# Four graph layers on 128 graphs, one core: a new order for fill and drain, the last transposition on TensorE, early statistics in the last layer

## Chip, cores and metric

One core of one Trainium2 chip. The metric is the device time in microseconds of one execution of the whole program; less is better.

## What is computed

`x` is (128 graphs, 128 nodes, 512 features) float32, `adj` a (128, 128) weighted adjacency shared by all graphs. Four layers follow each other, each with a residual and a layer normalisation `LN` over the 512 features:

```python
# layer 0
x = LN(x + (adj @ x) @ weight + bias)
# layer 1
q, k, v = x @ Wq.T, x @ Wk.T, x @ Wv.T
rel = adj.T * (q @ k.T)                       # per graph, 128 x 128
x = LN(x + (rel / norm(rel, axis=2)) @ v)
# layer 2
h = x @ W;  s1, s2 = h @ a[:512], h @ a[512:]
att = softmax(leaky_relu(s1[:, :, None] + s2[:, None, :], 0.2) * adj, axis=2)
x = LN(x + elu(att @ h + beta * h))
# layer 3: A = adj @ x, C = adj @ x + b; the maximum over the second index of relu(A + (C - A))
x = LN(x + relu(max over features of (adj @ x) + b))
```

In layer 3 the same adjacency stands for both weights, so what is added to `x` is one number per node and graph.

## The kernel before

The 128 graphs are worked in 32 groups of four. Nodes lie on the 128 partitions; a group's `x` is a 128 x (4, 512) tile. For each group the functions `layer0` to `layer3` put pieces of work, closures of a few instructions, into one list with a written time each (`emit`, `each`); the list is sorted by these times at the end, and that is the program order of all engines. The times are in slots, 28 for a group; the table `TABLE` holds them for an ordinary group, `FIRST` overrides them for groups 0 and 1, and `LAST` for the last three groups (29, 30, 31), there in microseconds counted from the start of group 31's middle product. The wrapper `InOrder` keeps each engine's instructions in program order, so an engine that waits holds up all that stands behind it in its queue. All instructions issued through the wrapper carry line 26 in the profile; tiles tell them apart.

The big products (256 or 512 wide) go through seven-product block multiplication: `left_factors` makes four sums of the left operand on GpSimd, `weight_blocks` four of the weight on VectorE, `product` takes seven steps of four 128x256 matmuls each (eight records in the profile), and after each step `out` moves a result off PSUM, ScalarE for steps 1, 6, 5 and 4 of a fresh target, VectorE for 2, 7 and 3 (order 1, 2, 6, 5, 7, 3, 4). Steps 6, 7 and 4 go on adding in the PSUM region of step 1, step 3 in that of step 5, so each waits for the one before to be read. Tiles of a product are `r_y` (layer 0), `r_m` (x times M, with M = Wq' Wk held in `m_qk`), `r_v` (values) and `r_z` (layer 2). Other tiles: `p_y` adj times x, `p_rel` scores, `p_o` attention output, `p_z` layer 2's gathered rows, `p_a` layer 3's products, each in one of three PSUM banks; `c` layer 2's result, `m` its exponential, `mx` and `top` layer 3's maximum, `mean` and `r` its shift and scale, `wa` the two weight rows with which VectorE forms layer 2's s1 and s2 (`dots`, tile `scr`).

Start (lines 95 to 230): SP loads `adj`, the four graphs of group 0, Wq, Wk, Wv and small tensors; ScalarE's queue loads `w0`, `bias` and `w2`. TensorE transposes `adj`, ScalarE copies it to `adjT`. `prepare_0` makes the factors of w0, `prepare_qk` forms M with 16 plain 128x512 matmuls (`p_m`), `prepare_v` transposes Wv (`p_wv`), `prepare_dots` and `prepare_rows` make `wa`, `prepare_2` the factors of w2.

In layer 1 `rel` is transposed by VectorE in 32x32 blocks and 16 transfers on SP (`turn_rel`, `move_rel`). In layer 3 (`squares`, `top`, `spread`, `shift`, `apply`) ScalarE takes the sum of squares of x, adds `top` to x with a running sum, VectorE turns both sums into mean and variance, GpSimd raises to -1/2, ScalarE applies and SP stores. In group 31 layer 2's product is direct (`direct`, tile `c`, one 128x512 accumulation of four matmuls for each graph), and normalisation and storing go graph by graph. In the last two groups (`late`) s2 is spread over partitions by four TensorE transposes (`p_s`), in the others by a DRAM round trip.

Of the kernel before, what the change touches and what calls it, by code (L numbers as in the profile page):

```python
# [29 lines left out]
def kernel(  # L30
# [41 lines left out]
    G = 4  # L72
    NG = B // G
    assert B % G == 0 and K == 4

# [11 lines left out]
    def on_all(row, n):  # L87

        return bass.AP(tensor=row.tensor, offset=row.offset, ap=[[0, P], [1, n]])
# [6 lines left out]
    def load(g):  # L96
        x1[g] = data.tile([P, G, D], FP, tag="x1", name=f"x1_{g}", bufs=3)
        if g == 0:
            for b in range(G):
                nc.sync.dma_start(x1[g][:, b, :], x[b])  # L100
        else:
            sync.dma_start(x1[g], x[g * G : (g + 1) * G].rearrange("b n d -> n b d"))

    load(0)
    w0_sb = const.tile([P, K, D], FP)
    nc.scalar.dma_start(w0_sb, w0.rearrange("(k p) f -> p k f", p=P))
    bias_sb = const.tile([P, D], FP)
    nc.scalar.dma_start(bias_sb, on_all(bias0, D))

    wq_sb = work.tile([P, K, D], FP, tag="tv", name="wq_sb")  # L110
# [6 lines left out]
    w2_sb = const.tile([P, K, D], FP)  # L117
    nc.scalar.dma_start(w2_sb, w2.rearrange("(k p) f -> p k f", p=P))
    a_sb = data.tile([P, 2, D], FP, tag="x3", name="a_sb")
# [6 lines left out]
    bias_halves = {0: bias_sb[:, :H], 2: bias_sb[:, H:]}  # L126
    dve.tensor_tensor(bias_halves[2], bias_halves[2], bias_halves[0], ALU.subtract)

# [12 lines left out]
    pe.transpose(pt[:, :P], adj_sb, ident)  # L141
    act.copy(adjT, pt[:, :P])
    adj_b = adj_sb[:, None, :].to_broadcast([P, G, P])
# [8 lines left out]

    def weight_blocks(w, name, keep=0):


        def blk(kh, ch):
            return w[:, 2 * kh : 2 * kh + 2, H * ch : H * ch + H]

        t = const.tile([P, 3 + keep, 2, H], FP, name=f"t_{name}")
        t2, t3, t4 = t[:, 0], t[:, 1], t[:, 2]  # L160
        t1 = t[:, 3] if keep else blk(0, 1)
        dve.tensor_tensor(t3, blk(1, 1), blk(0, 1), ALU.subtract)
        dve.tensor_tensor(t2, t3, blk(0, 0), ALU.add)
        dve.tensor_tensor(t4, blk(1, 0), t2, ALU.subtract)
        dve.tensor_tensor(t1, blk(0, 1), blk(0, 0), ALU.subtract)
        return {1: blk(0, 0), 2: blk(1, 0), 3: blk(1, 1), 4: t4, 5: t1, 6: t2, 7: t3}

    bw = {}

    def prepare_0():  # L170
        bw["0"] = weight_blocks(w0_sb, "0")

    def prepare_qk(c):

        pm = bank(f"p_m{c}")
        for e in range(K):
            pe.matmul(
                pm,
                wq_sb[:, e, c * P : (c + 1) * P],
                wk_sb[:, e, :],  # L180
                start=(e == 0),
                stop=(e == K - 1),
            )
        act.copy(m_qk[:, c, :], pm)
        if c == K - 1:
            bw["m"] = weight_blocks(m_qk, "m")

    def prepare_v(c):
        pv = bank(f"p_wv{c}")
        for e in range(K):  # L190
            pe.transpose(pv[:, e * P : (e + 1) * P], wv_sb[:, e, c * P : (c + 1) * P], ident)
        act.copy(wvT[:, c, :], pv)
        if c == K - 1:
            bw["v"] = weight_blocks(wvT, "v")

# [16 lines left out]
    def prepare_rows():  # L212

        for i in range(2):
            for k in range(K):
                pe.transpose(
                    wa[:, i, k * P : (k + 1) * P],
                    col[:, i, k : k + 1].to_broadcast([P, P]),
                    ident,
                )  # L220
        dve.tensor_reduce(wa_sum, wa, AX.X, ALU.add, negate=True)
        dve.tensor_scalar(beta_i, ident, beta_sb, None, op0=ALU.mult)

    def prepare_2():
        bw["2"] = weight_blocks(w2_sb, "2", 1)

# [10 lines left out]
    def row(at, step, n=G):  # L237
        return [at + i * step for i in range(n)]
# [18 lines left out]

    FIRST = {0: dict(turn=row(20.4, 0.3)), 1: dict(y=row(-9.5, 0.3))}

    LAST = {  # L260
        NG - 3: dict(
            exp=[0.8, 1.5, 2.2, 11.0], elu=[9.7, 12.3, 14.6, 17.2], norm2=[19.5],
            apply2=row(21.0, 0.8), widen=[24.5, 27.1, 29.7, 32.3], top=[25.5, 28.0, 30.6, 33.2],
            stats3=[27.0, 29.9, 32.2, 35.8], norm3=[42.0], apply3=row(44.0, 0.8), store=[47.4],
        ),
        NG - 2: dict(
            scale=[5.6], apply1=row(24.3, 0.8), spread=[6.9], leaky=[7.4], weighted=[9.0],
            greatest=[10.5], exps=[11.2], divide=[13.6], turn_att=[18.3], with_beta=[18.9],
            gather=row(36.7, 0.9), z_sums=row(39.95, 1.3),
            z_w=[40.0, 41.8, 43.5, 45.2, 47.0, 49.4, 51.1], exp=[51.5, 52.2, 56.2, 58.6],  # L270
            elu=row(56.9, 2.3), norm2=[66.1], apply2=row(67.7, 0.8), widen=row(73.0, 0.86),
            top=[73.7, 74.6, 78.0, 78.9], stats3=row(79.8, 0.9), norm3=[83.4],
            apply3=row(84.8, 0.8), store=[88.2],
        ),
        NG - 1: dict(
            m=[0.0, 1.73, 3.46, 5.2, 7.4, 9.1, 10.8], scores=row(12.7, 0.9), masked=[16.4],
            squares=[17.2], turn_rel=[17.1], move_rel=row(18.0, 0.1), inverse=[20.0], v=[16.7, 18.4, 21.0, 22.7, 25.3, 27.9, 30.5],
            attend=row(33.2, 0.86), residual=row(34.1, 1.65), norm1=[40.65], dots=row(40.7, 1.53),
            scale=[47.0], apply1=row(47.5, 0.8), spread=[48.9], leaky=[49.4], weighted=[51.0],
            greatest=[52.4], exps=row(53.2, 0.6), divide=row(53.9, 0.6),  # L280
            turn_att=row(54.4, 0.6), with_beta=row(54.9, 0.6), gather=[55.2, 56.1, 60.5, 65.0],
            z_w=[57.0, 61.5, 66.0, 69.5], exp=[60.6, 65.0, 69.6, 73.2],
            elu=[66.3, 68.8, 71.3, 75.5], norm2=[68.5, 71.0, 73.5, 77.7],
            apply2=[70.0, 72.5, 75.0, 79.4], widen=[77.0, 77.9, 78.8, 80.5],
            top=[83.5, 84.4, 85.3, 87.0], stats3=[86.1, 87.9, 88.8, 89.7],
            norm3=[86.9, 88.7, 89.6, 90.5], apply3=[88.3, 90.1, 91.0, 91.9],
            store=[89.2, 91.0, 91.9, 92.8],
        ),
# [59 lines left out]

    def product(at, name, mul, s, w, c, fresh, begin=None, before=None):

# [35 lines left out]
        for n, i in enumerate(ORDER):  # L386
            if before is not None and i in (1, 5):
                emit(at[n] - 0.7, fill, REGION[i])
            emit(at[n], step, i)
            emit(at[n] + 0.72, out, i)  # L390
# [46 lines left out]
    def layer0(g, t):  # L437
# [18 lines left out]
        if g > 0:  # L456
# [3 lines left out]
        product(  # L460
            t["y_w"], f"y_{g}", by_rows, s, "0", rows_of(lambda: x1[g]), False, before=bias_halves
        )
# [4 lines left out]
    def layer1(g, t):  # L467
# [69 lines left out]
        def turn_rel():  # L537
            s["relB"] = work.tile([P, 2, Q, 2 * P // Q], FP, tag="relB", name=f"relB_{g}")
            s["relT"] = work.tile([P, 2, 2 * P], FP, tag="relT", name=f"relT_{g}")
            for b in range(G):  # L540
# [3 lines left out]
                )  # L544

        def move_rel(a):
            n = P // Q
            for q in range(Q):
                sync.dma_start(
                    s["relT"][q * n : (q + 1) * n, :, 2 * a * n : 2 * (a + 1) * n],  # L550
                    s["relB"][a * n : (a + 1) * n, :, q, :],
                )
# [18 lines left out]
        def residual(b):  # L571
# [9 lines left out]
            )  # L581
            stats(s, f"1_{g}", b, x2[g][:, b, :])

# [40 lines left out]
        emit(t["squares"][0], squares)  # L624
        emit(t["turn_rel"][0], turn_rel)
        each(t["move_rel"], move_rel)
        emit(t["inverse"][0], inverse)
        product(t["v"], f"v_{g}", by_rows, s, "v", rows_of(lambda: s["v"]), True, begin_values)
        each(t["attend"], attend)
        each(t["residual"], residual)  # L630
        each(t["dots"], dots)
        emit(t["scale"][0], scale_dots)
# [7 lines left out]
    def layer2(g, t):  # L640
# [4 lines left out]
        def spread():  # L645
            if late:
                p = bank(f"p_s2_{g}")
# [134 lines left out]
        def elu(b):  # L782
            if b == 0:
                x3[g] = data.tile([P, G, D], FP, tag="x3", name=f"x3_{g}")
            x = x3[g][:, b, :]
# [31 lines left out]
    def layer3(g, t):  # L817
# [47 lines left out]
        def store(i):  # L865
            for b in range(i * n, i * n + n):
                sync.dma_start(out[g * G + b], x3[g][:, b, :])

        n = G // len(t["store"])
        each(t["widen"], widen)  # L870
        for b in range(G):
            emit(t["widen"][b] - 0.1, squares, b)
        each(t["top"], top)
        each(t["norm3"], spread)
        for i in range(len(t["norm3"])):
            emit(t["apply3"][i * n] - 0.1, shift, i)
        each(t["apply3"], apply)
        each(t["store"], store)


    emit(-1, prepare_0)
    each(row(14.0, 1.0), prepare_qk)
    each(row(18.0, 0.1), prepare_v)
    each(row(29.2, 1.8), prepare_dots)
    emit(40.7, prepare_rows)
    emit(61.0, prepare_2)
    for g in range(NG):
# [33 lines left out]
```

## Time and profile before

| | us |
|---|---|
| three runs | 2187.71, 2188.13, 2185.8 (median 2187.71) |
| the profiled execution | 2185.83, its span 2184.1 |
| PE busy, share of the span | 2149.5, 98% |
| DVE / ACT / POOL busy | 1552.1 / 1127.9 / 716.3 |
| chain that ended last | PE 94%, DVE 3%, ACT 2% |

Matmuls are pipelined, so the step from the start of one to the start of the next is what counts, and the durations in the table of groups are longer than that step. The page's slices of the span show PE at 9 tenths or more in all but the first and the last slice. The times below are from the start of the span.

### The profile page before, as it was taken

Reading aid. Unit: us, or ns where it says so; the run is one execution under the profiler, and the core shown is the slowest. Engines: PE = TensorE matmul, PEld = TensorE weight load, DVE = VectorE, ACT = ScalarE, POOL = GpSimd, SP = SyncE. Lnnn points to the kernel's source line nnn. Section 1 sums busy time; section 2 is a strip of 40 time slices with the busy share of each in tenths; the row PEclk is TensorE's granted clock in tenths of the full one; section 3 lists DMA queues with packets and bytes.
Section 4 is the critical chain, followed back from the end, with each engine's and each line's share of the span. In section 5 each row is a group of like instructions: output and inputs, shape, how many; then the busy total and the mean of one; then the engine's idle time right before and its main releaser. Section 6 shows DMA issues by size and latency. Waiting matters only on the chain.

```text
span 2184.1 us, 31923 instructions
## 1 busy us (share of the span) xinstructions
PE 2149.5 (98%) x10839; PEld 1814.6 (83%) x10839; DVE 1552.1 (71%) x3411; ACT 1127.9 (52%) x2510; POOL 716.3 (33%) x585
## 2 busy tenths in 40 slices
PE   8999999999999999999999999999999999999996
PEld 6888888888888888888888888888888888888873
DVE  3666777777767767767767777767777767677776
ACT  3235455555455555455554455554555554555557
POOL 1223333233333333233323333333332333342321
PEclk9999999999999999999999999999999999999998
DMA  4022222222222222322221323222322222322101
GB/s 170 6 58 50 67 73 68 57 57 63 71 74 68 54 59 60 75 70 73 54 57 60 75 66 78 54 52 65 74 67 61 64 55 70 73 68 56 38 25 58
DMA packets 363537, 138.82 MB, mean 64 GB/s; under 512 B 304624, under 2 KB 320112, under 8 KB 363376
## 3 DMA queue, kind: packets, MB, share of 16 engines
q1 hardware_dynamic: 362176, 134.43, 24.4%
q10 hardware_dynamic: 1200, 2.36, 0.3%
q8 instruction: 87, 1.43, 0.3%
q14 instruction: 74, 0.61, 0.1%
HBM read 55.38 MB, written 41.48 MB: 44 GB/s over the span
## 4 chain that ended last, share of the span: by engine, by line
PE 94%; DVE 3%; ACT 2%; issue 0%; POOL 0%; DMA 0%; ACTq 0%; DVEq 0%
PE r_y L26 17%; PE r_m L26 17%; PE r_v L26 17%; PE r_z L26 17%; PE p_y L26 5%; PE p_z L26 5%; PE p_rel L26 5%; PE p_o L26 5%; PE p_a L26 5%; DVE x L26 1%; ACT x L26 1%; PE p_m L26 1%; DVE st L26 1%; DMA w_sb<-in_L_gnn_weight_dram 0%; DVE t L26 0%
## 5 line engine op out<-in xcount | busy, mean ns | idle before, releaser
L26 ACT ACTIVATE x<-x,nmean,rstd 128x512 f32<-128x512 f32 x384 | 285.6, 807 | 41.3 <-DVE nmean L26 38.0
L26 DVE BATCH_NORM_STATS2 st<-x 128x6 f32<-128x512 f32 x384 | 263.0, 685 | 8.7
L26 POOL TENSOR_TENSOR rstd<-ve,mhalf 128x4 f32<-128x4 f32 (+1 forms) x99 | 108.9, 1100 | 334.4 <-DVE ve L26 334.4
L26 DVE TENSOR_TENSOR x<-r_y,x 128x512 f32<-128x512 f32 x224 | 152.2, 680 | 92.5 <-PE r_y L26 82.5
L26 ACT COPY yT<-p_y 128x512 f32<-128x512 f32 x128 | 75.0, 586 | 192.5 <-PE p_y L26 192.5
L26 DVE TENSOR_REDUCE mx<-p_a 128x1 f32<-128x512 f32 x128 | 88.2, 691 | 105.3 <-PE p_a L26 102.4
L26 DVE SCALAR_TENSOR_TENSOR scr<-x,wa 128x512 f32<-128x512 f32 x256 | 162.3, 679 | 0.0
L26 ACT ACTIVATE x<-x,mean,r 128x512 f32<-128x512 f32 x128 | 97.1, 808 | 108.4 <-DVE mean L26 108.4
L26 POOL TENSOR_TENSOR rn<-n,mhalf 128x4 f32<-128x4 f32 x32 | 32.6, 1017 | 347.5 <-ACT sq L26 347.5
L26 PEld LDWEIGHTS p_y<-adjT,x 128*128 128x128 f32 x1024 | 135.0, 194 | 8.9 <-ACT adjT L26 2.6
L26 PEld LDWEIGHTS p_z<-eT,x 128*128 128x128 f32 x1024 | 134.0, 192 | 7.9 <-issue 1.0
L26 PEld LDWEIGHTS p_rel<-xT,tT 128*128 128x128 f32 x1024 | 134.1, 191 | 7.4 <-DVE tT L26 0.8
L26 DVE TENSOR_TENSOR tT<-r_m,tT 128x512 f32<-128x512 f32 x96 | 66.3, 691 | 102.4 <-PE r_m L26 97.9
L26 ACT COPY tT<-r_m 128x512 f32<-128x512 f32 x128 | 75.6, 591 | 121.3 <-PE r_m L26 121.3
L26 PE MATMUL p_y<-adjT,x 128*128 128x128 f32 x1024 | 135.8, 277 | 2.1 <-ACT adjT L26 2.1
L26 PE MATMUL p_rel<-xT,tT 128*128 128x128 f32 x1024 | 134.9, 275 | 0.6 <-DVE tT L26 0.6
L26 PE MATMUL p_z<-eT,x 128*128 128x128 f32 x1024 | 134.7, 275 | 0.1
L26 ACT COPY zT<-p_z 128x512 f32<-128x512 f32 x128 | 73.8, 576 | 117.5 <-PE p_z L26 117.5
L26 PE MATMUL p_a<-x,adjT 128*128 128x512 f32 x256 | 126.3, 597 | 5.8 <-DVE mx L26 4.4
L26 POOL TENSOR_TENSOR s_y<-yT 128x512 f32<-128x512 f32 x32 | 41.1, 1284 | 276.1 <-ACT yT L26 276.1
L26 PE MATMUL p_o<-v,relT 128*128 128x512 f32 x256 | 130.5, 593 | 0.3 <-ACT v L26 0.3
L26 ACT COPY v<-r_v 128x512 f32<-128x512 f32 x128 | 74.1, 579 | 108.3 <-PE r_v L26 108.3
(135 smaller groups left out, 5214.7 us busy)
## 6 DMA issues: line engine op xcount, KB each, us to landing
out_dram<-x SPq DMA_DIRECT2D x128, 256.0 KB, 2.1
x<-in_x_dram SPq DMA_DIRECT2D x31, 1024.0 KB, 7.5
xT<-xB SPq DMA_DIRECT2D x480, 64.0 KB, 2.3
relT<-relB SPq DMA_DIRECT2D x512, 16.0 KB, 1.8
s<-s2d SPq DMA_DIRECT2D x30, 256.0 KB, 5.1
eBd<-eB SPq DMA_DIRECT2D x30, 256.0 KB, 2.0
eT<-eBd SPq DMA_DIRECT2D x120, 64.0 KB, 2.0
w_sb<-in_L_gnn_weight_dram ACTq DMA_DIRECT2D x1, 1024.0 KB, 5.7
```

What stands on the lines that cost most here:

```text
L26: return lambda *args, **kw: self.tc.keep_in_program_order(op(*args, **kw))
```

## The change

At the start: `bias` moves to SP's queue between the second and third graph, w2 to SP's behind Wv; VectorE instead of ScalarE copies `adjT`; eight matmuls of the identity follow adj's transposition (`p_warm`); the bias copy for the first product comes earlier (`lead`); M is formed by the seven-step product, with sums of Wq on GpSimd and factors of Wk on VectorE in a borrowed buffer; the factors of each weight are four pieces with times of their own; the preparation pieces and the pieces of groups 0 and 1 get new times; group 0's s2 is spread by TensorE. At the end: new times for the last three groups; group 31's `rel` is turned by four TensorE transposes and one ScalarE copy; its layer 1 statistics come after all four residuals; its layer 2 output takes the `xB` buffer; in groups 30 and 31 layer 3's statistics are taken of x itself, ahead of `top` (adding one number to a row moves its mean and not its variance), so ScalarE's squares and sums fall away, and `top` is formed on VectorE.

```diff
+                if b == 1:
+                    nc.sync.dma_start(bias_sb, on_all(bias0, D))
...
-    nc.scalar.dma_start(bias_sb, on_all(bias0, D))
...
-    nc.scalar.dma_start(w2_sb, w2.rearrange("(k p) f -> p k f", p=P))
+    nc.sync.dma_start(w2_sb, w2.rearrange("(k p) f -> p k f", p=P))
...
-    act.copy(adjT, pt[:, :P])
+    dve.tensor_copy(adjT, pt[:, :P])
+
+    warm = bank("p_warm")
+    for i in range(WARM):
+        pe.matmul(warm[:, :P], ident, ident, start=True, stop=True)
...
-    FIRST = {0: dict(turn=row(20.4, 0.3)), 1: dict(y=row(-9.5, 0.3))}
+    FIRST = {
+        0: dict(stats0=row(15.8, 0.02), norm0=[15.95], apply0=row(18.0, 0.1), turn=row(20.4, 0.3),
+                dots=row(57.8, 0.1), scale=[58.9], spread=[61.6]),
+        1: dict(y=row(-9.5, 0.3), y_sums=row(-4.0, 0.1), apply0=row(18.0, 0.1), turn=row(20.3, 0.3),
+                x_sums=row(22.5, 0.5)),
+    }
...
+        def turn_last():
+            p = bank(f"p_relT_{g}")
+            for b in range(G):
+                pe.transpose(p[:, b * P : (b + 1) * P], s["rel"][:, b, :], ident)
+            s["relT"] = work.tile([P, 2, 2 * P], FP, tag="relT", name=f"relT_{g}")
+            act.copy(
+                s["relT"].rearrange("p h (n j) -> p h j n", j=2),
+                p.rearrange("p (h j n) -> p h j n", h=2, j=2),
+            )
...
-            stats(s, f"1_{g}", b, x2[g][:, b, :])
+            if g < NG - 1:
+                stats(s, f"1_{g}", b, x2[g][:, b, :])
...
-            if late:
+            if late or g == 0:
...
+                    x3[g] = work.tile([P, G, D], FP, tag="xB", name=f"x3_{g}")
...
+        def top_late(b):
...
+            dve.tensor_reduce(mx, s["a", b], AX.X, ALU.max)
+            tp = s["top"][:, b : b + 1]
+            dve.tensor_scalar(tp, mx, b3_sb, 0.0, op0=ALU.add, op1=ALU.max)
+
+        def shift_late(i):
...
+            dve.tensor_tensor(m, s["mv"][:, sl, 0], s["top"][:, sl], ALU.add)
+            dve.tensor_tensor(m, s["top"][:, sl], m, ALU.subtract)
+            dve.tensor_tensor(m, m, s["r", i], ALU.mult)
...
+            each(t["stats3"], lambda b: stats(s, f"3_{g}", b, x3[g][:, b, :]))
+            each(t["norm3"], spread_early)
+            each(t["top"], top_late)
...
-    each(row(14.0, 1.0), prepare_qk)
-    each(row(18.0, 0.1), prepare_v)
-    each(row(29.2, 1.8), prepare_dots)
-    emit(40.7, prepare_rows)
-    emit(61.0, prepare_2)
+    weight_blocks(row(-1, 0), "0", w0_sb)
+    weight_blocks([11.85, 11.86, 12.85, 12.86], "k", wk_sb, 1, "x2")
+    qk = {"qT": wq_sb}
+    left_factors(row(12.0, 0.1), qk, "qT", "s_x", "q", 1)
+    product(row(14, 1, 7), "qk", by_rows, qk, "k", rows_of(lambda: m_qk), True)
+    weight_blocks([19.8, 19.81, 20.9, 20.91], "m", m_qk)
+    each(row(21.0, 0.1), prepare_v)
+    each([29.8, 30.4, 34.0, 34.5], prepare_dots)
+    weight_blocks(row(36.0, 1.0), "v", wvT)
+    emit(49.0, prepare_rows)
+    weight_blocks(row(72.3, 0.1), "2", w2_sb, 1)
```

Of the last groups' written times: group 29's last three `p_a` (`widen`) move from 27.1, 29.7, 32.3 to 54.9, 55.0, 59.3; group 30's `z_w` from 40.0 to 51.1 becomes 37.2 to 48.3; group 31's `elu` goes from 66.3, 68.8, 71.3, 75.5 to 56.5, 62.0, 67.5, 70.9 and its `top` from 83.5 to 87.0 to 69.86 to 77.0.

## The prediction

> **What bounds the kernel now.** First the busy time of each engine in three stages (columns: length, busy time of PE, PEld, DVE, ACT and POOL with instruction counts, granted clock, DMA share, GB/s):
>
> ```profile
> 0.00:160.00 160.00, 149.91 (x735) 122.02 (x736) 83.41 (x170) 48.57 (x99) 40.23 (x37) 0.99 0.26 79
> 160.00:2079.00 1919.00, 1918.74 (x9762) 1636.50 (x9761) 1395.82 (x3053) 1014.16 (x2262) 654.64 (x525) 1.00 0.26 64
> 2079.00:2184.10 105.10, 80.87 (x346) 56.08 (x344) 72.84 (x190) 65.16 (x149) 21.41 (x23) 0.93 0.09 34
> ```
>
> The reader is to see that TensorE idles 10.1 us in the fill, 0.3 us in 1919 us of steady work, and 24.2 us in the drain. The program order of groups 3 to 28 is the same in both kernels on every engine, so whatever TensorE gains before 160 us reaches the end undiminished, and only fill and drain can change. Next the start: granted clock by stage, TensorE's waits before 50 us, and the order of time.
>
> ```profile
> 6.00:9.00 3.00, 0.93 (x6) 0.54 (x5) 0.46 (x3) 1.55 (x2) 0.00 (x0) 1.00 0.95 302
> 9.00:12.00 3.00, 3.00 (x16) 3.00 (x15) 2.56 (x4) 0.76 (x2) 0.00 (x0) 0.50 1.05 405
> 12.00:13.00 1.00, 1.00 (x9) 1.00 (x9) 0.00 (x0) 0.41 (x1) 0.00 (x0) 0.80 1.05 389
> ```
> ```profile
> PE p_y L26 <- ACT adjT L26: 2.1, 1, 2.1
> PE p_wv L26 <- ACT wvT L26: 1.9, 1, 1.9
> PE r_y L26 <- ACT r_y L26: 1.2, 1, 1.2
> ```
> ```profile
> 6.43 0.39 ACTq L118 DMA_DIRECT2D w_sb<-in_L_gnn_W_dram  x1
> 6.85 1.28 ACT L26 ACT_TABLE_LOAD   x1 [6.85 <-DMA w_sb<-in_L_gnn_weight_dram]
> 8.14 0.27 ACT L26 COPY adjT<-p_adjT 128x128 f32<-128x128 f32 x1
> 8.46 5.47 PE L26 MATMUL p_y<-adjT,x 128*128 128x128 f32 x32 [2.07 <-ACT adjT L26]
> 27.29 13.90 PE L26 MATMUL p_m<-wk_sb,wq_sb 128*128 128x512 f32 x32
> ```
>
> ScalarE's third load (w2) waits until w0 has landed; behind it stand the table load and the adjT copy, and TensorE waits for that copy. It goes cold meanwhile: eight p_y records take 1.7 us at clock 0.50 and 0.87 later. Last the end, in order of time and in the chain of waits:
>
> ```profile
> 2141.94 0.68 DVE L26 SCALAR_TENSOR_TENSOR x<-c,x 128x512 f32<-128x512 f32 x1
> ...
> 2179.07 0.16 DVE L26 TENSOR_TENSOR mean<-mean,r 128x1 f32<-128x1 f32 x1 [0.59 <-POOL r L26]
> ```
> ```profile
> 2180.40 0.70 ACT x L26
> ```
>
> From the first ELU of group 30 (2141.94) to the last shift (2179.07) it is VectorE and ScalarE that set the time, 37.1 us; 5.0 us more pass until the end.
>
> **What the Trainium skill says.** "TensorE: Matmul & The Clock Gate", section "What's actually happening": half rate by default, full rate after about 3.4 us of sustained work. The trace agrees: 0.50 in 9 to 12 us, full from about 12.4, 3.9 us after p_y began. The same page, "Architectural detail", calls the queues of ACT and DVE strict FIFOs; the adjT wait above is one. "SBUF — State Buffer", section "SBUF: two separate sides", calls the port pair of VectorE and GpSimd an exclusive lock: the four factors of w2 at 111.9 us took 1.42, 1.64, 1.64 and 0.68 us with GpSimd running, against 0.69 alone.
>
> **Fill, part by part.** Prices are steps from start to start: one product step (eight records of 128x256) 1.725 us, eight 128x128 records 0.865, four transposes 0.43, two 128x512 records 0.86, a 128x512 copy on ACT 0.5 to 0.58, a sum on POOL 1.25, on DVE 0.61 to 0.73.
>
> 1. adjT by DVE (which idles until 8.5), w2 moved to SP, bias to SP between x[1] and x[2]. p_adjT ends at 6.39, adjT is there at about 6.7. The 16 warm records run 6.2 to 8.0 (0.108 each at the clock p_adjT had: its record took 0.27, as at full clock). x[0] had landed at 7.3 (it released SP's wv load), x[1] at 9.0. So p_y runs from 8.0 at full clock, paced by x: last block 10.6 to 11.5. Bounds: 0 to 1.9 us later if the clock drops all the same; bias in front of x[2] and x[3] at 390 GB/s costs x[3] at most 0.7.
> 2. The bias copy goes ahead of yT[3] (lead 4.4) and waits for bias; behind it on ACT is yT[3], for which POOL waits. In before bias landed at 8.5; now at 9 to 9.6; the copy's turn is 11.4: hidden. r_y starts at 11.95 (before 15.10) and ends 12.1 later at 24.05 (27.1).
> 3. M = Wq'Wk as a seven-step product: 12.1 instead of 13.8 (32 records by 0.43). Its sums on POOL (four by 1.25, 17.7 to 22.8, behind y's) and wk's factors on DVE (four by 0.7 to 1.64, between x sums) are done by 26.4, before their steps at 27.5 and later; wk landed at 18.5 before, 14 to 19 now.
> 4. p_y of group 1 goes inside this product, the turns of x and Wv alternate behind it: 3.46+1.73+1.73. Nine ACT copies by 0.58 feed three banks, TensorE waits about 1.1. x of group 1 (before: issued 13.84, landed 12.2 later) is needed at 32.7: hidden, though SP's loads now queue behind w0's landing. So r_m of group 0 starts at 24.05+19.0+1.1 = 44.1 (50.43).
> 5. r_m, r_y, r_v of groups 0 and 1 follow with the same work; wa (0.87) only moves; the turn of s2 for group 0 adds 0.43. The pauses of 1.34 (106.6), 1.73 (about 117) and 0.43 (123.9) go: group 0's dots now stand after tT's first sum, the four factors of w2 (6.4 with GpSimd) move past 132 us, where nmean of group 2 stands behind them; ScalarE cannot take that apply before 140.8 in any case (it copies v until then). Starts: r_m(1) 90.0 (97.23), r_y(2) 106.0 (114.50), r_v(2) 121.8 (132.69).
>
> Sum 10.9; some 15 handovers of 0.05 to 0.1 are left out, so I take **10.0**, bounds 6 and 11.
>
> **Drain, part by part**, on the clock of before (r_m of group 31 at 2079.06).
> 1. Two sums of tT now stand before the ELU on DVE: p_rel ends at 2095.4 (2096.25). Layer 3 of group 29 leaves r_v: four p_a by 0.86 and the pauses 0.16, 0.63, 0.56 go. rel by four transposes (0.43) and one ACT copy replaces 16 SP issues (10.9 us from 2099.6), which would land about 2112.5; p_o now starts at 2108.4 (2113.9). p_o ends 2111.9, r_z starts 2115.3 (2122.3).
> 2. Here some is given back. Statistics of all four blocks (four by 0.82) and rstd (1.02) stand before s_z on POOL: step 3 of r_z waits until 2120.0. Eight dots (4.9) stand before its second sum on DVE, four applies before its third copy on ACT: step 4 at 2122.2, step 5 at 2125.2 (0 to 1 more by the shared port; I take 0.4). The p_a of group 29 fills one gap. p_z of group 31 starts at 2131.6 (2139.5), the first ELU at 2134.0 (2141.94).
> 3. The tail on DVE: eight ELUs with statistics by 2.27 = 18.2, eight early statistics by 0.82 = 6.6, eleven maxima by 0.64 = 7.0 (three of group 29 moved here), eight tops by 0.2, five shifts by 0.6, group 29's small steps 1.0, other small ones 2.5: 39.9. Waits: the first ELU of group 31 stands on DVE before group 30's last two, and its exp stands on ACT behind a copy of p_z's third block, itself behind c_0 and two p_a (about 1.5); two statistics wait for an apply (0.4 and 0.9). 42.7 in all against 37.1, last shift at 2176.7 less 0.7 for small steps that overlap = 2176.0 (2179.07). Four applies instead of one then follow: end at 2176.0+4 by 0.72+3.0 (last apply's end 2181.1 to 2184.1) = 2181.9.
> The squares and sums that leave ACT (8 by 0.6+0.7+0.3 = 12.8) are worth little by themselves: ACT is no longer last. The output of group 31 in the xB buffer costs nothing: that buffer was last read by xT's transfers, tens of us before.
>
> Drain gain 2.2, bounds -3 and +9. Sum 12.2: the profiled span 2184.1 becomes 2171.9. The median of the runs stands 3.6 above that span; I take the difference from it: 2187.7-12.2 = **2175.5**.
>
> **Rivals.**
> A. The tail is not VectorE's: if the 7.9 us by which the first ELU comes earlier pass through (small steps overlap, statistics fill waits that exist anyway: before, DVE had some 7 us of waits there), 10+8 = 18: 2169.7. Against: the 12 us of work added to that tail exceed these waits.
> B. The fill gives half: clock cold through p_y (1.9), bias late, banks slower; 6, and nothing in the drain: 2181.7. For: the 405 GB/s of that stage leave DMA no slack.
> C. Slower: the tail's loops run one after another. Each block of group 31 goes DVE statistics, POOL 0.55, apply 0.81, DVE statistics 0.82, POOL 0.55, shift 0.6 and small steps, 3.9 us; both queues are in order. Four loops in series add 15.6-2.8 = 12.8 to the tail: 2188.3. It decides from about 15 us of VectorE idle between first ELU and last shift. Against: the written order puts an ELU or a maximum into each loop.
>
> **How the numbers follow.** Likeliest 0.55 (2171 to 2180), A 0.20, B 0.19, C 0.06. Under 0.2% (4.4 us, about what a measurement of this kernel tells from no change) lie part of B and C. Faster 0.89, same 0.06, slower 0.05. Range 2168.5 to 2182.5 reaches to A and B.
>
> **What would show it.** Right: p_y from 8.0 at clock 1.00; r_y from 12; M's product 12 us long; r_m(0) at 44; r_v(2) at 122; then the drain's first ELU 55 us after r_m(31), last shift 97 after it, VectorE busy over 90% between. Wrong: clock 0.50 at 8 to 11; pauses before M's steps; a last shift under 92 us (A) or over 107 (C) after r_m(31).

## The result, and the profile after

The changed kernel takes 2174.1 us (median, 2173.83 to 2174.47) against 2187.48 in the same session: a ratio of 0.994, 95% interval 0.9923 to 0.9957. The forecast was 2175.5. The profiled span is 2172.0 (forecast 2171.9, before 2184.1). Below, the fill is the stretch up to 160 us, r_m(31) the start of group 31's r_m, and the drain what follows it; times with a plus sign are counted from r_m(31).

Busy time by stage, columns as in the table of before (length; PE, PEld, DVE, ACT, POOL; granted clock; DMA share; GB/s), with the stages cut at the start of group 31's r_m, now 2069.0:

```profile
0.00:160.00 160.00, 158.02 (x832) 136.25 (x833) 97.19 (x200) 50.50 (x103) 50.58 (x46) 1.00 0.25 78
160.00:2069.00 1909.00, 1908.82 (x9709) 1627.49 (x9708) 1387.66 (x3032) 1011.76 (x2258) 648.95 (x521) 1.00 0.26 64
2069.00:2172.00 103.00, 82.24 (x349) 56.60 (x348) 75.79 (x198) 53.19 (x110) 21.29 (x23) 0.93 0.08 31
9.00:12.00 3.00, 3.00 (x28) 2.86 (x26) 1.01 (x3) 1.98 (x4) 0.00 (x0) 1.00 1.06 408
```

TensorE's idle time in the fill went from 10.1 to 2.0 us, and the clock between 9 and 12 us from 0.50 to 1.00. From group 31's r_m to the end it is 103.0 us, where it was 105.0. TensorE's waits before 50 us, and the start in order of time:

```profile
PE p_wv L26 <- ACT wvT L26: 0.3, 1, 0.3
PE r_y L26 <- ACT r_y L26: 0.3, 1, 0.3
```
```profile
1.21 1.28 ACT L26 ACT_TABLE_LOAD   x1 [1.21 <-PEq L992]
6.73 0.29 DVE L26 COPY adjT<-p_adjT 128x128 f32<-128x128 f32 x1 [5.86 <-PE p_adjT L26]
8.31 3.74 PE L26 MATMUL p_y<-adjT,x 128*128 128x128 f32 x32
12.32 3.72 PE L26 MATMUL r_y<-w_sb,yT 128*128 128x256 f32 x16 [0.27 <-ACT r_y L26]
24.52 3.62 PE L26 MATMUL r_qk<-wk_sb,wq_sb 128*128 128x256 f32 x16
```

The wait for adjT is gone, those for Wv's copies and for the bias are 0.3 each (before: 1.9 and 1.2). The end, in order of time (first the first ELU of group 30 and of group 31, then the last shift and the four applies behind it):

```profile
2123.37 0.68 DVE L26 SCALAR_TENSOR_TENSOR x<-c,x 128x512 f32<-128x512 f32 x1
...
2130.32 0.69 DVE L26 SCALAR_TENSOR_TENSOR x<-c,x 128x512 f32<-128x512 f32 x1 [2.21 <-ACT m L26]
...
2165.83 0.16 DVE L26 TENSOR_TENSOR mean<-mean,r 128x4 f32<-128x4 f32 x1
2166.03 2.92 ACT L26 ACTIVATE x<-x,mean,r 128x512 f32<-128x512 f32 x4 [0.56 <-DVE mean L26]
```

The first ELU comes 54.3 us after r_m of group 31 (before 62.9), the last shift 96.8 (100.0). Of the 8.6 us won by the first ELU, 3.2 are left at the last shift, and 2.1 at the end, because four applies follow that shift where one did.

### The profile page after: what moved, and what is told of

Its sections match the earlier page's. It is cut to its first block, busy times and chain, and to the rows that moved or that the text cites. A ratio compares the mean times of both kernels' runs of the same rounds, so it can differ in the third digit from the quotient of the medians.

```text
span 2172.0 us, 31973 instructions
## 1 busy us (share of the span) xinstructions
PE 2149.1 (99%) x10887; PEld 1820.3 (84%) x10887; DVE 1560.6 (72%) x3429; ACT 1115.4 (51%) x2470; POOL 720.8 (33%) x589
## 4 chain that ended last, share of the span: by engine, by line
PE 97%; DVE 2%; ACT 0%; POOL 0%; issue 0%; ACTq 0%; POOLq 0%; DVEq 0%
PE r_m L26 18%; PE r_y L26 18%; PE r_v L26 18%; PE r_z L26 17%; PE p_rel L26 5%; PE p_y L26 5%; PE p_o L26 5%; PE p_z L26 5%; PE p_a L26 5%; PE r_qk L26 1%; DVE st L26 1%; DVE x L26 0%; DVE mx L26 0%; PE first_r L26 0%; ACT x L26 0%; PE c L26 0%
## 5 line engine op out<-in xcount | busy, mean ns | idle before, releaser
L26 DVE BATCH_NORM_STATS2 st<-x 128x6 f32<-128x512 f32 x392 | 268.3, 685 | 9.7 <-ACT x L26 1.1
L26 DVE TENSOR_REDUCE mx<-p_a 128x1 f32<-128x512 f32 x128 | 88.3, 690 | 99.6 <-PE p_a L26 96.8
L26 DVE TENSOR_TENSOR tT<-r_m,tT 128x512 f32<-128x512 f32 x96 | 66.3, 691 | 96.9 <-PE r_m L26 94.2
```

The lines of the kernel that those rows point to most:

```text
L26: return lambda *args, **kw: self.tc.keep_in_program_order(op(*args, **kw))
```

## The experiments

All medians stand against 2174.1 (changed) or 2187.3 to 2187.5 (before, in every session; its 17 runs in the last one from 2184.1 to 2189.0). The fill's gain can be read at r_m(31); "rest" is what follows until the end of the profiled span.

| run | median us | span | r_m(31) | rest |
|---|---|---|---|---|
| before / changed | 2187.5 / 2174.1 | 2184.1 / 2172.0 | 2079.06 / 2069.04 | 105.0 / 103.0 |
| fill_only | 2177.79 | 2176.5 | 2069.89 | 106.6 |
| no_warm | 2174.39 | 2172.4 | 2069.40 | 103.0 |
| adjT_on_act | 2174.33 | 2172.5 | 2069.47 | 103.0 |
| start_as_before | 2176.45 | 2173.2 | 2070.22 | 103.0 |
| bias_late | 2175.74 | 2173.7 | 2070.70 | 103.0 |
| m_plain | 2180.65 | 2178.7 | 2075.70 | 103.0 |
| rel_by_dma | 2175.05 | 2173.1 | 2069.52 | 103.6 |
| exp_first | 2173.42 | 2172.0 | 2070.17 | 101.8 |
| late_statistics | 2176.92 | 2174.6 | 2069.03 | 105.6 |
| end_order | 2170.83 | 2168.9 | 2069.10 | 99.8 |
| before_kept_warm | 2186.02 | 2183.9 | 2078.85 | 105.0 |
| before_all_warm | 2184.55 | 2182.8 | 2077.77 | 105.0 |

Differences of up to 1 us at r_m(31) need care. The start of p_adjT lay between 5.6 and 6.6 us in these profiles (TensorE's first six matmuls, tile `first_r`, which no run changed, stand ahead of it and took 4.4 to 5.5), and the unchanged steady work from r_v of group 2 to r_m(31) took 1946.2 to 1947.3.

### The fill alone

```diff
-    LAST = {NG - 3: dict(exp=[0.8, 10.5, 13.0, 18.0], ...
+    LAST = {NG - 3: dict(exp=[0.8, 1.5, 2.2, 11.0], ...
...
-        if g < NG - 2:
+        if True:
             squared = t.get("squares3", [v - 0.1 for v in t["widen"]])
```

The rest of this edit puts back the other written times of groups 29 to 31, the turn of `rel` by transfers, and group 31's layer 1 statistics and output buffer, all as before.

> The new fill with the drain as it was before (written times of the last three groups, rel of group 31 turned by VectorE and transfers, layer 3 on ScalarE everywhere). Theory (the fill's 10 us reach the end, the drain is worth 2): r_m of group 31 starts at 2069.0 +- 0.3, from there to the end 105.0 as before, profiled span 2174.1, the median 2.0 above that of the changed kernel and 10 to 11.5 below that before. Rival (fill and drain interact, the drain alone carries more than 2): median 4 or more above the changed kernel.

r_m(31) came at 2069.9, so the fill does carry over (r_y had already begun 0.35 us later than in the changed kernel). The rest took 106.6 instead of 105.0, and the median lies between the two expectations. The order of TensorE's work is that of before; its drain is the same to 0.1 us until 60.3 us after r_m(31). Then the clock differs. In order of time, first this run, then before, and the granted clock of this run:

```profile
2129.46 0.30 PE L26 MATMUL p_eT<-ident,e 128*128 128x128 f32 x1 [1.72 <-DVE rs L26]
2130.23 0.44 PE L26 MATMUL p_eT<-ident,e 128*128 128x128 f32 x1 [0.47 <-DVE rs L26]
2130.47 1.92 PE L26 MATMUL p_z<-eT,x 128*128 128x128 f32 x8
```
```profile
2138.61 0.30 PE L26 MATMUL p_eT<-ident,e 128*128 128x128 f32 x1 [1.72 <-DVE rs L26]
...
2139.52 1.06 PE L26 MATMUL p_z<-eT,x 128*128 128x128 f32 x8
```
```profile
2131.00:2134.00 3.00, 3.00 (x18) 3.00 (x18) 0.66 (x4) 0.62 (x2) 0.00 (x0) 0.60 0.00 0
```

After a pause of 1.72 us eight records take 1.92 us; in the profile of before, after the same pause, they took 1.06. By the fourth p_eT TensorE is 1.5 us behind before, nearly all of the 1.6 by which the rest is longer. Such a fall of the granted clock behind a pause is called a clock drop below. So a profiled span holds an element of chance that the prediction had not reckoned with. The last two experiments take it up.

### The start, part by part

No warming matmuls:

```diff
-    WARM = 8
+    WARM = 0
```

> The changed kernel without the eight warming matmuls. Theory (without them TensorE idles from 6.7 to 8.3 us and the clock drops, as it did before after 2.1 us of idling): clock about 0.50 from 9 to 12 us, p_y takes about 5.5 instead of 3.74 us, r_y starts at about 14.0 instead of 12.3, and the end comes 1.7 later. Rival (the clock holds over an idle time of 1.6 us, or p_y is paced by the arrival of x at any clock): r_y at 12.3, the end within 0.3.

The rival holds. In order of time:

```profile
7.38 2.05 PE L26 MATMUL p_y<-adjT,x 128*128 128x128 f32 x16 [0.38 <-DVE adjT L26]
9.93 2.05 PE L26 MATMUL p_y<-adjT,x 128*128 128x128 f32 x16 [0.50 <-DMA x<-in_x_dram]
```

p_y starts a microsecond earlier, at full clock, and waits for x instead; r_y starts at 12.25, and the end is within 0.4 us. With adjT this early the pause before p_y is 0.38 us, and the clock holds; the warming matmuls only fill the time until x is there. Next ScalarE copies adjT again:

```diff
-    dve.tensor_copy(adjT, pt[:, :P])
+    act.copy(adjT, pt[:, :P])
```

> The changed kernel with adjT copied by ScalarE again, w2 and bias left on SP's queue. Theory (the copy was late only because ScalarE's queue stood still at its third load, and that load is gone): table load stays at about 1.2 us, copy at 6.7, p_y at 8.3 as before it, the end within 0.3. Rival (ScalarE itself is late at the copy, by its table load or by its wait): p_y starts 1 to 2 us later and the end follows by as much.

```profile
6.31 0.27 ACT L26 COPY adjT<-p_adjT 128x128 f32<-128x128 f32 x1 [3.81 <-PE p_adjT L26]
```

The theory holds: the table load is at 1.22, the copy at 6.31, the end as changed. The engine of the copy doesn't matter once w2 and the bias have left ScalarE's queue. Then the whole first part is undone, but for the early bias copy:

```diff
-    WARM = 8
+    WARM = 0
...
-                if b == 1:
-                    nc.sync.dma_start(bias_sb, on_all(bias0, D))
...
+    nc.scalar.dma_start(bias_sb, on_all(bias0, D))
...
-    nc.sync.dma_start(w2_sb, ...)
+    nc.scalar.dma_start(w2_sb, ...)
...
-    dve.tensor_copy(adjT, pt[:, :P])
+    act.copy(adjT, pt[:, :P])
```

> The changed kernel with the first part of the fill undone as a whole: bias and w2 on ScalarE's queue, adjT copied by ScalarE, no warming matmuls; the early bias copy and all else stay. Theory (this part is worth the 3.15 us by which r_y was to start earlier): table load at 6.9, p_y from 8.5 at clock 0.50, r_y at 14.0 to 15.1, the end 1.7 to 2.9 later. Its difference to the kernel that only lacks the warming says what the two queue moves add: 0 to 1.2. Rival (most of the first part is the early bias copy, which stays): end within 0.8.

```profile
8.55 3.84 PE L26 MATMUL p_y<-adjT,x 128*128 128x128 f32 x32 [1.49 <-ACT adjT L26]
```

TensorE waits for adjT again, but in the profiled execution the clock stayed up and r_y started at 12.66. The other three executions had spans 1.3 to 1.7 us longer (2174.5 to 2174.9). That is the size of a clock drop; no trace of them shows it. The median is 2.35 above the changed kernel, as the theory has it, but in the profile without a drop r_y lies only 0.3 behind (the 1.2 at r_m(31) are mostly the variation of the steady part): on this evidence, most of what the first part buys is that TensorE has no such pause. Next the bias copy goes back to its old place:

```diff
-            lead=4.4 if g == 0 else 0.7,
+            lead=0.7,
```

> The changed kernel with the bias copy of group 0's first product at its old place behind the last yT copy (lead 0.7 instead of 4.4). Theory (r_y of group 0 waits for that copy, which then ends one copy later): r_y starts at 12.8 to 13.0 instead of 12.3, and the end is 0.5 to 0.7 later. Rival (the sums on GpSimd, which wait for the last yT, gain by as much as the copy loses): end within 0.2.

```profile
13.69 1.56 PE L26 MATMUL r_y<-w_sb,yT 128*128 128x256 f32 x6 [1.17 <-ACT r_y L26]
```

The wait of 1.17 us is that of the kernel before; it was 0.27. The early copy is worth 0.9 us, more than the theory's 0.5 to 0.7. The end is later still, 1.7 at r_m(31): p_y also began 0.5 late here, behind longer `first_r`, p_adjT and p_warm matmuls that the edit doesn't touch, and the steady work took 0.3 longer.

### M by plain matmuls

```diff
+    def prepare_qk(c):
...
-    weight_blocks([11.85, 11.86, 12.85, 12.86], "k", wk_sb, 1, "x2")
...
-    left_factors(row(12.0, 0.1), qk, "qT", "s_x", "q", 1)
-    product(row(14, 1, 7), "qk", by_rows, qk, "k", ...)
+    each([14.0, 15.75, 17.5, 19.25], prepare_qk)
```

> The changed kernel with M formed by 16 plain matmuls again, in the same place (group 1's p_y and the turns between them). Theory (TensorE is what the fill waits for there, so its own work counts): M takes 13.8 instead of 12.1 us, r_m(0) starts at 46.1 instead of 44.4, the end comes 1.7 later; the four sums on GpSimd and four factors on VectorE that fall away are worth nothing. Rival (the stretch is set by the copies of ScalarE or by the arrival of Wk): r_m(0) within 0.5 of 44.4, the end too.

The loss is far larger than either expectation has it: r_m(0) starts 2.5 us later and r_m(31) 6.7. In order of time:

```profile
38.71 3.70 PE L26 MATMUL p_m<-wk_sb,wq_sb 128*128 128x512 f32 x8 [1.29 <-ACT yT L26]
...
53.15 3.58 PE L26 MATMUL r_m<-s_x,t_m 128*128 128x256 f32 x8 [2.61 <-POOL s_x L26]
```

M now shares the three PSUM banks with p_y, which costs 1.3 us, and group 1's last p_y moves behind it; GpSimd therefore sums y of group 1 late (44.1 instead of 39.3), and x of group 0 behind it, for which r_m waits 2.61. The eight records after that pause took 3.58 us instead of 1.89 (clock 0.50 between 53.15 and 56 us). 2.5+2.6+1.7 is the whole loss. So the run doesn't isolate the product's 1.7 us: it shows that the product and the order around it are one piece.

### The drain, part by part

```diff
-            squares=[17.2], turn_rel=[20.3], inverse=[19.0],
+            squares=[17.2], move_rel=row(18.0, 0.1), turn_rel=[17.1], inverse=[19.0],
...
-        if g < NG - 1:
+        if True:
             emit(t["turn_rel"][0], turn_rel)
             each(t["move_rel"], move_rel)
```

> The changed kernel with group 31's rel turned by VectorE blocks and 16 transfers again, all written times as changed but for those of the turn and its transfers, which are the old ones. Theory (the transfers land about 33.4 us after r_m(31), so p_o waits for them): p_o starts 3.5 to 4.1 later than at +29.35, TensorE idles for it, and the first ELU and the end come 2 to 4 later. Rival (p_o's start is not what sets the tail, since r_z's steps wait for GpSimd and VectorE anyway): p_o later, first ELU and end within 0.7.

The rival holds: +0.5 at the first ELU. In order of time:

```profile
2087.78 10.19 SPq L26 DMA_DIRECT2D relT<-relB  x16
2099.28 3.68 PE L26 MATMUL p_o<-v,relT 128*128 128x512 f32 x8 [0.70 <-DMA relT<-relB]
```

The transfers are issued from 18.3 us after r_m(31), not from 20.6 as before: the new order puts `rel` itself ahead of an ELU on VectorE. They delay p_o by 0.4 us (+29.76 instead of +29.35). The turn on TensorE is worth half a microsecond; of the 6 us by which p_o comes earlier than before (+35.3), 5.5 are the work of the order.

```diff
-            z_w=[51.8, 56.1, 60.4, 63.9], exp=[55.3, 59.6, 63.9, 67.5],
+            z_w=[51.8, 56.1, 60.4, 63.9], exp=[55.1, 59.6, 63.9, 67.5],
```

> The changed kernel with one written time altered: the exponential of group 31's first block stands ahead of the copy of p_z's third block on ScalarE, not behind it. Theory (the tail is VectorE's, and its one large pause of 2.21 us is due to that order): the pause before the third ELU goes, first ELU stays at +54.3, last shift at 94.6 to 95.2 instead of 96.8 after r_m(31), the end 1.6 to 2.2 earlier. Rival (later pauses take its place, since the chain through p_z, c and exp of group 31's later blocks sets the pace): last shift moves by less than 0.7.

```profile
2137.33 0.69 DVE L26 BATCH_NORM_STATS2 st<-x 128x6 f32<-128x512 f32 x1 [1.41 <-ACT x L26]
```

The pause of 2.21 us is gone, a later one has grown from 0.41 to 1.41, and the last shift comes at +95.6, between the two expectations: about half of the pause could be saved on VectorE alone, the other half came back as a wait for ScalarE.

```diff
-        if g < NG - 2:
-            squared = t.get("squares3", ...)
+        if True:
+            squared = t.get("stats3" if g >= NG - 2 else "squares3", ...)
...
-            norm3=[62.0, 67.45, 74.2, 76.6]
+            norm3=[71.0, 74.35, 76.25, 77.75]
```

Group 30's statistics and its shift, and group 31's applies and stores, get other written times to match.

> The changed kernel with layer 3 of groups 30 and 31 in the old way (sum of squares and running sum with top on ScalarE, five small steps on VectorE, GpSimd after them), its small steps written behind other work of VectorE. Theory (the tail is VectorE's; this takes 8 by 0.87 statistics and 8 by 0.2 tops from it and adds some 20 small steps of 0.1 to 0.2): VectorE's busy time between first ELU and last shift falls by about 5 us, last shift 3 to 5 us earlier. Rival (ScalarE gets 8 by 0.7+0.7+0.6 = 16 us more in a stretch where it now works 20 of 42, and its round trip enters the chain): last shift 0 to 5 us later, with VectorE waiting for ScalarE's sums.

Busy time between 2123.4 and 2166.0 us, first changed, then this run, and waits of VectorE in this run:

```profile
2123.40:2166.00 42.60, 29.23 (x70) 11.79 (x68) 36.80 (x104) 20.34 (x36) 7.63 (x11) 0.89 0.11 44
```
```profile
2123.40:2166.00 42.60, 30.75 (x70) 12.35 (x68) 28.98 (x83) 32.19 (x75) 6.58 (x10) 0.83 0.11 43
```
```profile
2150.45 0.15 DVE L26 TENSOR_SCALAR mean<-sum 128x1 f32<-128x1 f32 x1 [2.20 <-ACT x L26]
...
2161.30 0.15 DVE L26 TENSOR_SCALAR mean<-sum 128x1 f32<-128x1 f32 x1 [3.02 <-ACT x L26]
```

The window cuts off this run's last 2.4 us: up to its own last shift VectorE is busy for 30.0 us, 6.8 less than as changed. Yet the last shift comes 2.6 us later (+99.4), because VectorE waits 7.5 us for ScalarE's sums and 3.7 for GpSimd. The rival holds, in the one written order that was tried. The tail is not set by VectorE's load alone. Last, the exponential moved ahead as in exp_first, together with another order of the last 15 us:

```diff
-            top=[74.3, 74.9, 76.2, 77.7], stats3=row(75.7, 0.05), norm3=[75.95],
-            apply3=row(79.0, 0.8), store=[82.0],
+            top=[74.3, 74.9, 75.5, 76.2], stats3=row(75.0, 0.05), norm3=[75.2],
+            apply3=row(76.3, 0.01), store=[76.55],
...
-            top=[69.86, 73.25, 75.5, 77.0],
+            top=[69.86, 73.25, 77.0, 77.7],
...
```

> The kernel with the exponential moved ahead, and the written order of the last 15 us altered: group 30's statistics, maxima, shift and its four applies and stores come before group 31's last two maxima, so that one apply follows the last shift, not four. Theory (VectorE's queue sets the last shift whatever the order within it, and what follows it is cut from 2.9+3.0 to 0.8+3.0 us): last shift at 95 to 96 after r_m(31), the end 99.0 to 100.0 after it instead of 101.8 with the exponential alone and 103.0 as changed; median 2 us below that with the exponential alone. Rival (the stores, four of 256 KB at the end in either order, set the end): the end within 0.7 of that with the exponential alone.

```profile
2161.04 3.63 ACT L26 ACTIVATE x<-x,mean,r 128x512 f32<-128x512 f32 x5 [5.85 <-DVE mean L26]
2164.98 0.81 ACT L26 ACTIVATE x<-x,mean,r 128x512 f32<-128x512 f32 x1 [0.31 <-DVE mean L26]
```

The last shift stays at +95.6 (the kernel with the exponential moved alone has it there too), the applies of group 30 run beside VectorE's last work, and one follows. The rest is 99.8 us, the median 2170.83: 3.3 below the changed kernel, 0.9922 of the time before (0.9909 to 0.9936). This version beats both.

### The clock in the kernel before

The first of two additions to the kernel before:

```diff
                 s["p"] = bank(f"p_eT_{g}")
+                if g == NG - 1:
+                    for _ in range(8):
+                        pe.matmul(s["p"][:, :P], ident, ident, start=True, stop=True)
```

> The kernel before with one addition: eight 128x128 matmuls of the identity in front of group 31's first p_eT, where TensorE waits 1.72 us for VectorE. Theory (in most executions of the kernel before the clock drops at this pause, which costs the records that follow some 1.5 us; the changed kernel has no pause of over 0.9 us before its last products): the median falls by 1 to 1.7 from 2187.4 to about 2186, and the spread of 4 to 5 us narrows. Rival (the spread comes from elsewhere, the start or the transfers): median within 0.5 of 2187.4, or later by the 0 to 0.2 of the added matmuls.

The median fell by 1.5, but the spread is still 3.5 us (2184.3 to 2187.8), and with a ratio of 0.9995 (0.9986 to 1.0003) this alone decides nothing. Its profile shows why. At the start the clock stayed up after a wait of 1.68 us, and M began 1.65 us earlier than before; yet r_m(0) started at 50.41, as before (50.43). In order of time, first this run, then before:

```profile
8.44 3.84 PE L26 MATMUL p_y<-adjT,x 128*128 128x128 f32 x32 [1.68 <-ACT adjT L26]
...
42.80 0.66 PE L26 MATMUL p_wv<-ident,wv_sb 128*128 128x128 f32 x4 [1.94 <-ACT wvT L26]
43.29 5.46 PE L26 MATMUL p_y<-adjT,x 128*128 128x128 f32 x32
```
```profile
44.45 0.66 PE L26 MATMUL p_wv<-ident,wv_sb 128*128 128x128 f32 x4 [1.93 <-ACT wvT L26]
```
```profile
44.00:48.00 4.00, 4.00 (x23) 4.00 (x23) 3.69 (x7) 1.48 (x4) 0.00 (x0) 0.59 0.00 0
```

The last line is the granted clock of this run from 44 to 48 us. This time the clock fell at the pause in front of the fourth p_wv, and 32 records took 5.46 instead of 3.83 us. So all three pauses are filled, besides the above:

```diff
+    warm = bank("p_warm")
+    for i in range(8):
+        pe.matmul(warm[:, :P], ident, ident, start=True, stop=True)
...
+        if c == K - 1:
+            for _ in range(8):
+                pe.matmul(wa[:, 0, :P], ident, ident, start=True, stop=True)
```

> The kernel before with eight 128x128 matmuls of the identity in each of its three pauses of 1.7 to 2.1 us: between p_adjT and p_y at the start, in front of the fourth p_wv, and in front of group 31's first p_eT. Theory (each such pause drops the clock in some executions and not in others, at about 1.65 us a drop; that is the spread of the kernel before, and the part of the gain beyond the two profiled spans): no drop, r_m(0) at 48.8, profiled span 2182.2 to 2182.8, median at the low end of the kernel before, 2184.0 to 2184.6, spread under 1.5 us. Rival (the spread and the excess of the median over the profiled run have another source): median within 0.7 of 2187.5 or 2186.0, spread of 3 us or more.

```profile
43.50 3.83 PE L26 MATMUL p_y<-adjT,x 128*128 128x128 f32 x32
...
48.99 1.34 PE L26 MATMUL r_m<-xT,m_qk 128*128 128x256 f32 x5
```

r_m(0) starts at 48.99, the span is 2182.8, the median 2184.55, and the 13 runs lie within 0.7 us (2183.99 to 2184.70), where the kernel before spreads over 4.9: the theory holds. Idle matmuls alone take 2.9 us off, a ratio of 0.9989 (0.9981 to 0.9997).

The times of single runs say the same. But for one at 2189.8, all recorded times of the kernel before lie in four groups: 2184.1 to 2184.7, 2185.7 to 2186.2, 2187.0 to 2188.1 and 2188.5 to 2189.0. The mean granted clock noted with them is 0.997 in the first group, 0.996 in the second, 0.995 or 0.996 in the third and 0.994 in the fourth. Three pauses with none, one, two or three drops would give four such groups. With one pause filled the highest group is missing, and with all three filled only the lowest is left.

## Why the prediction held, and where it did not

**The sum.** Fill 10.0 forecast, 10.02 measured (r_m(31)); drain 2.2 and 2.08; span 2171.9 and 2172.0. The mechanism, TensorE's gain before 160 us passing through the steady part, is shown by the table of stages and by fill_only. That both come out within 0.15 us is in part luck: the steady part alone varies by 1.1 us between profiles, the profile of before happened to hold one clock drop, and two errors in the drain nearly cancel (the first ELU came 0.6 earlier than forecast, and the tail behind it took 0.5 longer).

**The step from span to median** is what was off. It took the 3.6 us between the profiled span and the median of before over to the new kernel; there it is 2.1. The profiled execution of before had one clock drop of about 1.65 us, its median execution about 1.8 of them by an estimate from the runs, (2187.47-2184.55)/1.65. The new order has no pause over 0.9 us until its last products, and its runs lie within 0.6 us. That accounts for the 1.4 us by which the forecast was high. One pause of 3.17 us remains in front of those last products, with half clock behind it (0.50 between 2152 and 2155 us), where VectorE is busy for 2.8 of 3 us; what it costs was not tried:

```profile
2148.98 3.48 PE L26 MATMUL p_a<-x,adjT 128*128 128x512 f32 x4 [3.17 <-ACT x L26]
```

**Fill, step 1.** r_y started at 12.32, forecast 11.95. The gain of 2.8 us there is a clock drop that did happen in the profile of before (about 1.65), the early bias copy (0.9), and 0.2 to 0.3 of everything else. The bound "0 to 1.9 us later if the clock drops all the same" took the warming matmuls to be what keeps the clock up. They were not needed: without them p_y is paced by x, and the clock holds in the profile of no_warm. The bias copy was called hidden, rightly; its 0.9 us gain stood unnamed in the sum.

**Fill, steps 3 and 4.** From M's start to r_m(0) 19.9 us, forecast 20.1 (19.0 and 1.1): the pauses at p_wv are 0.3, not 1.1, and the steps took about 0.5 more than summed. The price of 1.7 for M's product alone was not isolated.

**Fill, step 5.** r_v of group 2 at 122.6, forecast 121.8 and before 132.7; the pauses named did go (the second is 1.56 in the trace, not 1.73). The 0.8 us are the handovers, for which the sum had set aside 0.9. The four factors of w2 had taken 5.4 us, not 6.4, and GpSimd ran beside the first three only; neither enters the sum.

**Drain, step 1.** p_o came at +29.35, as forecast (its old start is +35.3; the 2113.9 that the forecast names is a weight load). The reason given for part of it failed: the transfers would not have landed 33 us after r_m(31) in the new order but 29.7, since the sums and `rel` moved too. A DMA step was priced with the issue time of the old order.

**Drain, step 2.** First ELU +54.3, forecast +54.9.

**Drain, step 3.** Last shift +96.8, forecast +96.9, with the wait of group 31's first ELU (2.2, forecast 1.5) in its place. But VectorE was busy 36.8 of 42.6 us, 86% and not the 90% named, and that the squares and sums that leave ACT "are worth little by themselves" is wrong, as far as late_statistics shows: with them back on ScalarE, and VectorE relieved, the last shift came 2.6 us later. The load on VectorE was summed rightly: outside its waits the tail took 39.1 us, forecast 39.2 (39.9 less the overlap of 0.7), and the waits came to 3.3, forecast 2.8. What the new load replaced, the round trip from maximum over ScalarE to VectorE, was not priced: of the 37.1 us of the tail before, 8.3 were waits of VectorE ("some 7" in the forecast), so the change traded 5.0 us of waits for 10.3 us of work. Rival A had the right sense that the tail is not VectorE's load only, and no more: the tail grew from 37.1 to 42.5 us all the same. Rivals B and C did not occur.

## What to carry to other kernels

Read a drain from its last shift or last store backwards before counting an engine's load: here two changes of written order, with no work removed, were worth 3.3 us, more than the TensorE turn and the drain's gain as changed. Here a pause of 1.7 to 2.1 us on TensorE cost about 1.65 us more in the work behind it, in some executions only; so compare medians and spreads and not two profiles, and close such pauses by order or fill them. When a transfer is replaced, price it with the issue time that it would have in the new order.

## What was not expected of the hardware

Near two microseconds the length of a pause does not decide by itself whether TensorE's clock drops. The same pause of 1.72 us, in the same order of work, was followed by a drop in the profile of fill_only and not in that of before. Profiled pauses of 1.72 (fill_only), 1.94 (before_kept_warm), 2.07 (before) and 2.61 us (m_plain) were followed by a clock of 0.5 to 0.6; pauses of 1.17 (bias_late), 1.49 (start_as_before), 1.68 (before_kept_warm), 1.72 and 1.93 (both before) and 1.81 us (in front of group 31's c, in before, fill_only and both fillings) were not. A drop cost 1.5 to 1.7 us. What decides stays open. The Trainium skill, "TensorE: Matmul & The Clock Gate", section "What's actually happening", has the monitor's window run freely, which would fit such a scatter, though no run here shows the window itself. The same section has the clock fall after an idle window of about 3.4 us, and here four shorter pauses, the shortest about half of that, were enough.
